# The down weights of a decoder's last feed-forward: all eleven unpacked from the start of the cross attention in front of it, ahead of the loads of the gate and up tiles

## The chip, the cores and the metric

The kernel runs on one core of a Trainium2 chip. A core has five engines with a queue of instructions each, which run in the order of their queues and wait for one another by semaphores: TensorE (PE, matrix products and transposes), VectorE (DVE), ScalarE (ACT), GpSimd (POOL) and SyncE (SP, which here only issues the transfers between memory and the core's buffers). The metric is the device time of one execution in microseconds, and lower is better: the median of several executions, 1584.54 us for the kernel before (three executions, 1584.25 to 1585.16).

## The reference, cut to what matters

A decoder of two layers with post-norm works on four batches of 512 rows by 512 columns in float32. Six stages follow one another, and each ends with a residual sum and a layer norm. The change touches the weights of the sixth stage, and moves their preparation beside the fifth.

```python
def _L1_xattn_ref(hidden_states, memory_tokens, memory_mask):        # stage E
    scores = jnp.einsum('bsd,bmd->bsm', hidden_states, memory_tokens) * scale
    scores = jnp.where(memory_mask[:, None, :], scores, neg_inf)
    attn = jax.nn.softmax(scores, axis=-1)
    readout = jnp.einsum('bsm,bmd->bsd', attn, memory_tokens)
    ...

def _dequant_fp4(packed_i32, scales_f16, group_size):                # group_size 128
    nib = w[:, :, None] >> shifts & jnp.uint32(15)
    vals = _FP4_LUT[nib.astype(jnp.int32)].reshape(out_f, in_p * 8)
    s_full = jnp.repeat(s, group_size, axis=1)
    return vals * s_full

def _L1_ffn_ref(x, gate_up_packed, gate_up_scales, down_packed, down_scales):   # stage F
    w_gu = _dequant_fp4(gate_up_packed, gate_up_scales, GROUP_SIZE)  # 2816 x 512
    w_down = _dequant_fp4(down_packed, down_scales, GROUP_SIZE)      # 512 x 1408
    gate_up = jnp.einsum('bsh,oh->bso', x, w_gu)
    gate, up = (gate_up[..., :I], gate_up[..., I:])                  # I = 1408 = 11 x 128
    h = jax.nn.silu(gate) * up
    y = jnp.einsum('bsi,hi->bsh', h, w_down)
    rms = jnp.sqrt(jnp.mean(y * y, axis=-1, keepdims=True) + EPS)
    return y / rms

x = _layernorm(x + _L0_attn_ref(...), axis=-1)     # A
x = _layernorm(x + _L0_xattn_ref(...), axis=-1)    # B
x = _layernorm(x + _L0_ffn_ref(...), axis=-1)      # C
x = _layernorm(x + _L1_attn_ref(...), axis=-1)     # D
x = _layernorm(x + _L1_xattn_ref(x, ctx_2048, mask_BxS2_bk0), axis=-1)   # E
x = _layernorm(x + _L1_ffn_ref(...), axis=-1)      # F
```

## The kernel before

The stages are called A to F, a task is one stage on one batch (E1 is the cross attention of layer 1 on batch 1), and the tasks run in the order A0 to A3, B0 to B3, and so on to F3. Between stages the rows go through memory: `finish` stores the four normed tiles of a task and `load_x` of the next stage loads them. A tile is 128 x 512.

**What sets the order.** Every task is a Python generator that writes instructions and yields after each step. `lanes` runs two tasks at once, step by step in turn, and starts the next when one is done or far enough. A `Pipe` holds work back: `later(n, f)` calls f n ticks later, so that an instruction is written only when its input is nearly there. The weights of later stages are prepared by background generators. `BESIDE` lists them as (first task, last task, key): after every step of the lanes, `step(n)` advances each listed generator by one step, from the start of its first task until the one behind the last has been started. If a task needs a weight that its generator hasn't written yet, `need` runs the generator on until it has. A scheduler then orders the instructions of each engine from what was written, with its own idea of when each is ready. It may move them past one another. `issue_after(i)` keeps what is written under it behind instruction i. `ahead` and `between` place the scalings of stage F and its norm.

**Buffers.** Pool `op` (tag o) has 69 tiles, `tp` (t) 13, `xp` (x) 12, `wp` (w) 4. An instruction or a load that takes a buffer waits until the last reader of its former content is done. In the SP queue such a wait holds all transfers behind it.

**High and low halves.** Products are made in three matmuls from a rounded high half and the rest: `split` copies the high half on ACT (L143) and subtracts it on DVE or POOL for the low half (L146). The names end in h and l: exh and exl are the halves of E's transposed input, p4h and p4l those of an unpacked down tile.

**Stage E (`l1_xattn`).** Per batch: loads of x and of the mask; the context in both layouts (ecT for the scores, ecn for the values, low halves on POOL); the mask's penalty (L1030, L1031); transposes of x (`ex`) with their splits; scores `es` (48 matmuls, lines 154 to 156); per score tile a minimum on DVE (L1041) and an exp on ACT (L1042); transposes of the weights (`ep`), the product with the values (`pv`), residual sum (L425) and norm statistics (L211, L212); and then the norm (L220, ACT's Ln and Exp, L174 to L176, four L235) and the stores.

**Stage D's end.** `merge` (L983, L984) joins D's results per tile, their transposes are `dF`, the output projection is `dy` and its sum L1001.

**Stage F (`l1_ffn`).** Per batch and per i of 11: eight scaled products `fg` (L1185), each scaled into a sum by ACT (L1133, L1137) or DVE (L1141); silu (L1149), the product with up (L1153), a split (fhh, fhl), and the accumulation `facc` over the down tile i (L1168). The gate and up codes were unpacked earlier (`l1_ffn_codes`, beside D1 to D3, key F0) and lie in memory (`gu_codes`); the down tiles are unpacked by `l1_ffn_weights`, key F.

**`l1_ffn_weights`.** It first finishes generator F0. Then, for each i of 11, it loads two gate and up tiles `gu` (pool o) from `gu_codes`, then the scales p4s and the packed down tile dn_p. Five ticks later (`F_LOAD`) `down` unpacks: `bits` is a shift (L1074) and a mask (L1075) on DVE, L1101 multiplies by the scale on DVE, and `split` copies p4h on ACT and subtracts p4l on POOL. Both halves stay in pool o until the end of F3: 22 buffers, and the 22 gu tiles likewise. In F, `need("F", ...)` at the start of each i asks that the down tile i + 1 has been written.

Of the kernel before, what the change touches and what calls it, by code (L numbers as in the profile page):

```python
# [12 lines left out]
F16 = mybir.dt.float16  # L13
BF16 = mybir.dt.bfloat16
I32 = mybir.dt.int32
# [6 lines left out]
B, S, D = 4, 512, 512  # L22
P = 128
# [8 lines left out]
LOG_EXP = "natural_log_exp_and_others"  # L32
D_NEXT = 7
B_NEXT = 13
F_LOAD = 5
CODES_EVERY = 3
F_SCALED, F_ACT, F_PAIR, F_DOWN = 1, 5, 3, 9
ORDER = "A0 A1 A2 A3 B0 B1 B2 B3 C0 C1 C2 C3 D0 D1 D2 D3 E0 E1 E2 E3 F0 F1 F2 F3"

BESIDE = [("A1", "A3", "C0"), ("A3", "B0", ("B", 0)), ("B0", "B2", "C"), ("C3", "D0", "D"), ("D1", "D3", "F0"), ("E2", "E2", "F")]  # L40


class Pipe:
# [25 lines left out]
class Net:  # L69
# [1023 lines left out]
    def l1_ffn_weights(self):  # L1093

        yield from self.bg["F0"]
        nc, a, bits = self.nc, self.a, self.bits
        pipe = Pipe()

        def down(w, sc):
            f = bits(w)  # L1100
            nc.vector.scalar_tensor_tensor(f, f, 2.0 ** 126, sc, ALU.mult, ALU.mult)  # L1101
            self.dn.append(self.split(f, "p4", lo_eng=nc.gpsimd))

        for i in range(11):
            for u in range(2):
                pipe.tick()
                self.gu[i, u] = self.o("gu", F32R)
                self.load(self.gu[i, u].bitcast(F32), self.gu_codes[i * 2 + u])
                yield
            pipe.tick()  # L1110
            sc = self.load(self.t("p4s", F16), a["dn_s"][i : i + 1, :].to_broadcast([P, 512]))
            pipe.later(F_LOAD, down, self.load(self.w("p4", I32), a["dn_p"][i]), sc)
            yield
        yield from pipe.drain()

    def l1_ffn(self, b):
        nc = self.nc
        pipe = Pipe()
# [57 lines left out]
            acc[t] = f  # L1176

        for i in range(11):
            self.need("F", lambda: len(self.dn) > min(10, i + 1))
            for u in range(2):  # L1180
                for g in range(4):
                    pipe.tick()
                    ps = self.pa("fg")
                    for n in range(2):
                        nc.tensor.matmul(ps, self.gu[i, u][:, g * P : (g + 1) * P], xT[g][n], start=n == 0, stop=n == 1)  # L1185
                    pipe.later(F_SCALED, scaled, i, u, g, ps)
                    yield
# [93 lines left out]
def body(tc, args, phases=range(6)):  # L1281
    with ExitStack() as ctx:
# [9 lines left out]
        def step(n):  # L1292
            if len(phases) == 6:
                for first, last, key in BESIDE:
                    if plain.index(first) < n <= plain.index(last) + 1:
# [74 lines left out]
```

## Time and profile before

| | us |
|---|---|
| median of three executions | 1584.54 (1584.25 to 1585.16) |
| the profiled execution | 1581.65 |
| its span, first to last instruction | 1580.0 |
| mean granted TensorE clock over it | 0.996 |
| PE busy, 1190 to 1280 (E1's tail to E3) | 84.03 of 90 |
| PE busy, 1280 to 1330 (F0) | 46.98 of 50 |
| L1074, L1075, L1101 each (medians of all on the tile) | 0.54, 0.49, 0.69 |
| p4h on ACT, p4l on POOL (medians) | 0.62, 1.30 |

The profile is of one execution; its times are counted from its first instruction, and the execution's own time is its span plus 1.65 us around it. E0 begins with its loads near 1137, its scores near 1144; E1's scores begin at 1183.3; F0's products run from about 1281. The unpacking of the eleven down tiles is spread from 1057 (first L1074) to 1321 (end of the last p4l).

In the views, a line of the timeline is start, length, engine, line of the kernel, operation, and out<-in by the program's names; brackets hold the idle time in front of it and what ended it. PEclk is the clock that the chip granted to TensorE, as a share of full speed. An engine that is not the one that the others wait for may idle for nothing.

### The profile page before, as it was taken

Reading aid. Unit: us, or ns where it says so; the run is one execution under the profiler, and the core shown is the slowest. Engines: PE = TensorE matmul, PEld = TensorE weight load, DVE = VectorE, ACT = ScalarE, POOL = GpSimd, SP = SyncE. Lnnn points to the kernel's source line nnn. Section 1 sums busy time; section 2 is a strip of 40 time slices with the busy share of each in tenths; the row PEclk is TensorE's granted clock in tenths of the full one; section 3 lists DMA queues with packets and bytes.
Section 4 is the critical chain, followed back from the end, with each engine's and each line's share of the span. In section 5 each row is a group of like instructions: output and inputs, shape, how many; then the busy total and the mean of one; then the engine's idle time right before and its main releaser. Section 6 shows DMA issues by size and latency. Waiting matters only on the chain.

```text
span 1580.0 us, 25595 instructions
## 1 busy us (share of the span) xinstructions
PE 1515.4 (96%) x8222; PEld 1090.1 (69%) x8222; DVE 1232.9 (78%) x2658; ACT 1021.3 (65%) x2208; POOL 666.2 (42%) x672
## 2 busy tenths in 40 slices
PE   8999999999999999899999999999999999999996
PEld 6888786444544674477777668777687777777875
DVE  6486589999976688777577797767786888888896
ACT  5333336988878877888696864969634445545554
POOL 6673663555535303430435323353225344344342
PEclk9999999999999999999999999999999999999998
DMA  7043344455214744653434445633436630020101
GB/s 255 29 157 124 113 154 132 149 173 176 78 48 123 224 137 133 201 185 134 134 102 118 104 141 148 171 97 92 125 123 222 233 110 12 24 81 1 54 1 53
DMA packets 134150, 192.31 MB, mean 122 GB/s; under 512 B 17265, under 2 KB 52081, under 8 KB 134017
## 3 DMA queue, kind: packets, MB, share of 16 engines
q1 hardware_dynamic: 129888, 182.23, 36.3%
q0 software_dynamic: 4128, 8.46, 2.2%
q8 instruction: 65, 1.06, 0.3%
q14 instruction: 69, 0.56, 0.1%
HBM read 117.75 MB, written 47.71 MB: 105 GB/s over the span
## 4 chain that ended last, share of the span: by engine, by line
PE 63%; DVE 17%; ACT 8%; issue 6%; DMA 3%; POOL 3%; SPq 0%; ACTq 0%; DVEq 0%; POOLq 0%
PE fg L1185 7%; PE facc L1168 5%; PE dT L933 3%; DVE fg L1141 3%; PE pg L687 3%; PE had L755 2%; PE dn L741 2%; DVE bsm L474 2%; PE pu L689 2%; ACT de L923 2%; PE bo L498 2%; PE do L953 2%; PE qk L156 2%; PE qk L155 2%; PE qk L154 2%
## 5 line engine op out<-in xcount | busy, mean ns | idle before, releaser
L1141 DVE SCALAR_TENSOR_TENSOR fg<-fg,gs,fg 128x512 f32<-128x512 f32 x220 | 163.2, 745 | 30.9 <-ACT fg L1133 15.3
L923 ACT ACTIVATE de<-de,dm 128x128 f32<-128x128 f32 (+3 forms) x256 | 142.9, 563 | 11.3 <-DVE dm L919 10.9
L1185 PE MATMUL fg<-fxh,gu 128*128 128x512 f32 x352 | 140.2, 398 | 6.1 <-DVE fg L1141 3.1
L919 DVE CUSTOM_DVE_ANT_0 de<-ds,negm,thr 128x128 f32<-128x128 f32 (+3 forms) x256 | 126.4, 546 | 19.4 <-PE ds L908 16.0
L482 POOL TENSOR_SCALAR be<-be,bsm 128x512 f32<-128x512 f32 x128 | 96.5, 766 | 103.8 <-DVE bsm L480 72.7
L1185 PE MATMUL fg<-fxl,gu 128*128 128x512 f32 x352 | 137.4, 390 | 0.1
L664 POOL TENSOR_TENSOR hl<-g,hh 128x512 fp32r<-128x512 f32 x64 | 83.4, 1309 | 110.2 <-ACT hh L663 90.2
L1145 POOL TENSOR_TENSOR fg<-fg,fg 128x512 f32<-128x512 f32 x44 | 60.2, 1367 | 139.6 <-DVE fg L1141 60.0
L476 ACT ACTIVATE be<-bs,bsm 128x512 f32<-128x512 f32 x128 | 87.3, 690 | 31.1 <-DVE bsm L474 29.2
L845 POOL TENSOR_TENSOR dql<-dqf,dqh 128x512 fp32r<-128x512 f32 x32 | 41.4, 1295 | 150.8 <-ACT dqh L844 150.6
L933 PE MATMUL dT<-ident,de 128*128 128x128 f32 x640 | 92.0, 280 | 8.5 <-ACT de L923 6.4
L933 PEld LDWEIGHTS dT<-ident,de 128*128 128x128 f32 x640 | 72.3, 142 | 28.3 <-ACT de L923 14.0
L1185 PEld LDWEIGHTS fg<-fxh,gu 128*128 128x128 f32 x352 | 66.0, 188 | 30.1 <-DVE fg L1141 12.7
L474 DVE TENSOR_REDUCE bsm<-bs 128x1 f32<-128x512 f32 x128 | 83.4, 672 | 0.0
L498 PE MATMUL bo<-bpT,cT 128*64 128x512 f32 x256 | 76.7, 618 | 2.4 <-ACT bpT L489 1.2
L248 PEld LDWEIGHTS bT<-ident,be 128*128 128x128 f32 x512 | 54.9, 141 | 34.0 <-issue 11.5
L248 PE MATMUL bT<-ident,be 128*128 128x128 f32 x512 | 73.2, 281 | 3.6 <-POOL be L482 2.1
L1185 PEld LDWEIGHTS fg<-fxl,gu 128*128 128x128 f32 x352 | 66.1, 188 | 12.8 <-DVE fxl L146 0.4
L352 POOL TENSOR_TENSOR z<-z,rope_cos 128x512 f32<-128x512 f32 x32 | 46.8, 1473 | 64.8 <-DVE zs L349 57.8
L1133 ACT ACTIVATE fg<-fg,gs 128x512 f32<-128x512 f32 x88 | 60.1, 684 | 20.6 <-PE fg L1185 20.4
L687 PE MATMUL pg<-qT,tb 128*128 128x512 bf16 x256 | 66.8, 381 | 4.5 <-ACT qT L649 2.8
L1159 POOL TENSOR_TENSOR fhl<-fg,fhh 128x512 fp32r<-128x512 f32 x44 | 58.5, 1331 | 29.5 <-ACT fhh L1158 29.3
(355 smaller groups left out, 4640.3 us busy)
## 6 DMA issues: line engine op xcount, KB each, us to landing
x<-x SPq DMA_DIRECT2D x176, 256.0 KB, 3.0
had_scratch<-hw SPq DMA_DIRECT2D x64, 256.0 KB, 2.3
z<-had_scratch SPq DMA_DIRECT2D x64, 256.0 KB, 5.8
stk<-dqh SPq DMA_DIRECT2D x192, 64.0 KB, 2.1
tw<-in_wg_t SPq DMA_DIRECT2D x32, 256.0 KB, 3.8
tw<-in_wu_t SPq DMA_DIRECT2D x32, 256.0 KB, 3.7
tw<-in_wd_t SPq DMA_DIRECT2D x32, 256.0 KB, 2.8
p<-in_gu_p SPq DMA_DIRECT2D x22, 256.0 KB, 3.1
```

What stands on the lines that cost most here:

```text
L248: self.nc.tensor.transpose(pt[:, i * P : (i + 1) * P], srcs[i][:, j * P : (j + 1) * P], self.ident)
L474: nc.vector.tensor_reduce(sm[:, h : h + 1], ps, AX.X, ALU.max, negate=True)
L476: nc.scalar.activation(e, ps, AF.Exp, bias=sm[:, h : h + 1], accum_out=sm[:, 2 + h : 3 + h])
L482: nc.gpsimd.tensor_scalar(es[h][i], es[h][i], sm[:, 4 + h : 5 + h], 1.0, ALU.mult, ALU.mult)
L498: nc.tensor.matmul(po[0][h * 64 : h * 64 + 64, :], cT[j][:, c : c + 64], pTs[h], start=j == 0, stop=j == NT - 1)
L664: nc.gpsimd.tensor_tensor(lo, g, hi.bitcast(F32), ALU.subtract)
L687: nc.tensor.matmul(pg, tern["wg_t"][k, c][:, m], qT[k], start=k == 0, stop=k == NT - 1)
L919: nc.vector.tensor_tensor_reduce(es[i], ps, self.negm[:, 384 - P * i :], -1.0, self.thr[:, i : i + 1], ALU.add, ALU.min, n4[:, i : i + 1])
L923: nc.scalar.activation(es[i], es[i], AF.Exp, bias=n4[:, i : i + 1], scale=-1.0, accum_out=den[:, hh * 4 + i : hh * 4 + i + 1])
L933: nc.tensor.transpose(pt[:, o + (i - j) * P : o + (i - j + 1) * P], es[i][:, j * P : (j + 1) * P], self.ident)
L1141: self.emitted["DVE"] = nc.vector.scalar_tensor_tensor(y[u], ps, s, y[u], ALU.mult, ALU.add)
L1185: nc.tensor.matmul(ps, self.gu[i, u][:, g * P : (g + 1) * P], xT[g][n], start=n == 0, stop=n == 1)
```

## The change

The generator for F's weights begins when E0 begins (before: E2) and is advanced until F0 has begun (before: until E3 has). It first loads and unpacks all eleven down tiles, one in two steps, with the unpacking two ticks behind the load (before: five), and no dn_p load is placed ahead of the instruction `self.stacked`, the last stacking transfer of D's projections written so far. When all are unpacked it loads the 22 gu tiles. In F, `need` now asks for the gu tile (i + 1, 1) instead of the down tile i + 1.

```diff
-F_LOAD = 5
...
-BESIDE = [..., ("D1", "D3", "F0"), ("E2", "E2", "F")]
+BESIDE = [..., ("D1", "D3", "F0"), ("E0", "E3", "F")]
...
         for i in range(11):
+            pipe.tick()
+            with self.tc.issue_after(self.stacked.ins):
+                w = self.load(self.w("p4", I32), a["dn_p"][i])
+            pipe.later(2, down, w, self.load(self.t("p4s", F16), a["dn_s"][i : i + 1, :].to_broadcast([P, 512])))
+            yield
+            pipe.tick()
+            yield
+        yield from pipe.drain()
+        for i in range(11):
             for u in range(2):
-                pipe.tick()
                 self.gu[i, u] = self.o("gu", F32R)
                 self.load(self.gu[i, u].bitcast(F32), self.gu_codes[i * 2 + u])
                 yield
-            pipe.tick()
-            sc = self.load(self.t("p4s", F16), a["dn_s"][i : i + 1, :].to_broadcast([P, 512]))
-            pipe.later(F_LOAD, down, self.load(self.w("p4", I32), a["dn_p"][i]), sc)
-            yield
-        yield from pipe.drain()
...
         for i in range(11):
-            self.need("F", lambda: len(self.dn) > min(10, i + 1))
+            self.need("F", lambda: (min(10, i + 1), 1) in self.gu)
```

`down`, `bits` and `split` are the same in both. So are the numbers of instructions on every engine: PE 8315, DVE 2643, ACT 1772, POOL 677, SP 840.

More of the change, by code (lines that the diff above doesn't have):

```diff
@@ L38 @@
 ORDER = "A0 A1 A2 A3 B0 B1 B2 B3 C0 C1 C2 C3 D0 D1 D2 D3 E0 E1 E2 E3 F0 F1 F2 F3"
-BESIDE = [("A1", "A3", "C0"), ("A3", "B0", ("B", 0)), ("B0", "B2", "C"), ("C3", "D0", "D"), ("D1", "D3", "F0"), ("E2", "E2", "F")]
+BESIDE = [("A1", "A3", "C0"), ("A3", "B0", ("B", 0)), ("B0", "B2", "C"), ("C3", "D0", "D"), ("D1", "D3", "F0"), ("E0", "E3", "F")]
 class Pipe:
```

## The prediction

> **What bounds the kernel now.** First the page: the share of each engine, then the chain of work that ended last.
>
> ```profile
> PE 1515.4 (96%) x8222; PEld 1090.1 (69%) x8222; DVE 1232.9 (78%) x2658; ACT 1021.3 (65%) x2208; POOL 666.2 (42%) x672
> ...
> PE 63%; DVE 17%; ACT 8%; issue 6%; DMA 3%; POOL 3%; SPq 0%; ACTq 0%; DVEq 0%; POOLq 0%
> ```
>
> TensorE is busy for 1515.4 of 1580.0 us, so all the time that any reordering can win lies in its idle 65 us, and a wait that it meets adds in full. The change touches the stretch from the last batch of the second self attention (D3) through the second cross attention (E0 to E3) to the first batch of the last feed-forward (F0). So next the busy times in ten-microsecond windows there (columns: window, length, PE, PEld, DVE, ACT, POOL busy with counts, granted clock, DMA share, GB/s).
>
> ```profile
> 1120.00:1130.00 10.00, 9.36 (x84) 6.91 (x82) 8.44 (x33) 9.05 (x29) 0.00 (x0) 1.00 0.03 7
> 1130.00:1140.00 10.00, 9.10 (x52) 4.01 (x52) 6.82 (x17) 4.82 (x14) 5.09 (x6) 0.83 0.65 230
> 1140.00:1150.00 10.00, 8.57 (x54) 7.07 (x54) 8.80 (x12) 4.71 (x9) 5.90 (x4) 1.00 0.91 284
> 1150.00:1160.00 10.00, 10.00 (x51) 8.23 (x50) 8.63 (x18) 7.26 (x16) 5.23 (x4) 1.00 0.24 84
> 1160.00:1170.00 10.00, 10.00 (x51) 8.32 (x50) 7.20 (x17) 0.59 (x1) 0.00 (x0) 1.00 0.01 2
> 1170.00:1180.00 10.00, 10.00 (x50) 8.40 (x49) 9.79 (x19) 3.01 (x7) 2.72 (x2) 1.00 0.33 113
> 1180.00:1190.00 10.00, 9.95 (x53) 8.15 (x52) 9.63 (x19) 4.42 (x10) 5.09 (x4) 1.00 0.51 179
> 1190.00:1200.00 10.00, 8.22 (x47) 6.40 (x45) 3.06 (x9) 4.85 (x11) 3.39 (x3) 1.00 0.93 317
> 1200.00:1210.00 10.00, 8.94 (x40) 6.95 (x41) 6.17 (x13) 8.89 (x18) 8.28 (x8) 1.00 1.02 380
> ...
> sum 210.00, PE 197.99 PEld 153.49 DVE 172.88 ACT 103.28 POOL 85.86; mean PE 9.43 PEld 7.31 DVE 8.23 ACT 4.92 POOL 4.09
> ```
>
> The reader is to see three things. PE idles 1.78 and 1.06 us in the two windows from 1190, while DVE has 6.94 and 3.83 us to spare. DVE is full from 1170 to 1190 (9.79 and 9.63), just before that idle time. And over 1120 to 1190, DVE has 70 - 59.31 = 10.7 us free in all. In F0, a window from 1280 to 1330 shows PE busy 46.98 of 50, an idle 3.02 us; the two stretches of 50 us behind it show only 0.25 and 0.46. Which operations PE waits for, from 1120 to 1340 (us in total, times, longest):
>
> ```profile
> PE ep L248 <- ACT ee L1042: 2.6, 5, 1.1
> PE dT L933 <- ACT de L923: 1.5, 3, 0.7
> PE es L154 <- DVE exl L146: 1.5, 2, 1.3
> PE fg L1185 <- ACT fg L1133: 1.3, 2, 0.9
> PE dF L248 <- DVE do L984: 1.2, 1, 1.2
> PE fg L1185 <- DVE fg L1141: 1.2, 2, 0.9
> ```
>
> Last, the timeline of DVE and ACT in these places (start, length, engine, line, operation, with the idle time before it):
>
> ```profile
> 1183.37 0.68 DVE L146 TENSOR_TENSOR exl<-ex,exh 128x512 fp32r<-128x512 f32 x1
> 1189.31 1.92 DVE L235 TENSOR_SCALAR x<-x,ln 128x512 f32<-128x512 f32 x4
> 1200.14 0.69 DVE L146 TENSOR_TENSOR exl<-ex,exh 128x512 fp32r<-128x512 f32 x1 [7.08 <-ACT exh L143]
> 1195.12 1.27 ACT L143 CAST ecnh<-ecn 128x512 fp32r<-128x512 f32 x2 [7.96 <-DMA ecn<-in_ctx]
> 1317.29 1.63 DVE L1101 SCALAR_TENSOR_TENSOR p<-p,p4s 128x512 f32<-128x512 f32 x1
> ```
>
> E1's first exl, the low half of its transposed input, starts at 1183.37 and PE's first score matmul that reads it at 1184.10: it is just in time. E1's tail then stalls on ACT, which stands for 7.96 us behind a late ecn load. In F0 an unpack step L1101 takes 1.63 us between the scaling steps L1141 that PE needs.
>
> **The change, part by part.** Nothing is added or removed: the instruction counts of all engines are equal, and only places change.
>
> *One set.* Unpacking one down tile costs, by the medians of the unpack tile p, DVE 0.541 (L1074) + 0.485 (L1075) + 0.689 (L1101) = 1.71 us, ACT 0.62 (p4h) and POOL 1.30 (p4l). Start to start, where they run back to back, the three DVE steps take 0.44 + 0.40 + 0.61 = 1.45.
>
> *What comes into 1120 to 1190 on DVE.* Before, the bit steps of tiles 1 to 4 ran at 1057.5 to 1066, their L1101 at 1158.9 to 1163.7, and tiles 5 to 11 from 1209.8 to 1317.3. In the changed program's order all 11 stand between D3's softmax and E1's first exl. So DVE gets 4 x 1.03 + 7 x 1.71 = 16.1 us (13.5 start to start) into a stretch with 10.7 us free: at least 16.1 - 10.7 = 5.4 must overflow (2.8 by the short durations). If only the larger gaps can be used (1.5 in 1120 to 1130, 2.6 between L1031 and the first L983 at 1141, 2.8 in 1160 to 1170) it is 16.1 - 6.9 = 9.2.
>
> *Where the overflow lands.* Three sets stand right in front of E1's exh and exl, with E0's layer norm (L220, ACT's Ln and Exp, L174 to L176), and E0's four L235 now come ahead of exl 2 to 4 instead of behind all four. Queued behind them on DVE are all of E1's scores; PE has nothing else to do there. E1's last exl ended at 1186.92, and PE read it some 1 us later (score matmuls start every 0.23 us there, the one at 1187.87 reads it at the latest); the norm and L235 in front of it, until 1191.2, are at most 4.3 - 1.0 = 3.3 more. Hence a PE delay of 5.4 to 9.2 + 3.3 = 12.5 us, or 2.8 if the short durations hold and the norm's steps fill gaps. I take **8.0**, nearer the low end, as E0 itself absorbs part of it. In this sum stands the extra L1101 ahead of E0's own second exl (0.8 us).
>
> *POOL beside DVE.* L1101 took 0.69 us alone and up to 1.63 beside POOL's work. In E0 it runs beside p4l as well, and so can stretch L235 (0.54 to 1.5). This is the reason for not taking the low end. [...]
>
> *The clock.* After the gaps around 1130 the granted clock was 0.62 in 1132 to 1134 and 0.53 in 1134 to 1136: 0.76 + 0.94 = 1.7 us lost. PE's pause at E1 may bring the same: 0 to 1.7, taken as **0.8**. [...]
>
> *What it wins.* E1's tail: the ecn loads stay where they are on SP (behind E0's x stores), while the scores come some 8 us later, so the exps are no longer late. PE idle 1.78 + 1.06 = 2.84, of which I take **2.4** back (bounds 2.0 and 2.84). E2 and E3: DVE loses the sets at 1209.8 to 1270; the PE idle there is small except 2.11 in 1250 to 1260, which has the same late ecn load as its cause and is not touched: **0.6** (0 to 2.0). F0: 3.02 idle against some 0.3 in the 50 us behind it; **2.4** (1.0 to 3.0). Together 5.4, bounds 3.0 and 7.8.
>
> *At nothing:* the bits taken out of 1057 to 1066 (PE is busy 19.98 of 20 there), and the DMAs. Eleven dn_p and p4s loads move ahead; on SP the dn_p loads 5 and 6 wait for POOL's p4l 1 and 2 to free a buffer, and E1's x and mask loads and E0's ecn loads stand behind them, at about 1150 instead of 1140. E0's ecn is used near 1174 and E1's x at 1181.7, so 24 and 30 us of cover hide it; gone, each us is one of PE. The 22 gu loads are all ahead of E3's context loads, and have until 1280.
>
> *Sum:* +8.0 + 0.8 - 5.4 = **+3.4 us** on the profiled execution (1581.65 us; span 1580.0 and 1.65 around it). That execution is 0.2% under the median of 1584.54; I carry the difference over: 1584.54 + 3.4 = **1587.9**.
>
> **The rivals.**
> *The sets fit in.* DVE's short durations hold, the gaps are filled, and exl comes 2.8 us late at most, half of it over PE's own shift in E0 (some 1.4 us of PE). Then +1.4 + 0 - 5.4 to -7.8, in the middle -5.2: 1579.3. For it: PE is 10.00 of 10 busy from 1150 to 1180, so DVE's work can slide behind it for long; F0's gain is plain in the rows. Against it: 9.79 and 9.63 from 1170.
> *A draw.* An overflow of 5 us pays for a relief of 5.4: 1584.1.
> *Late context loads*, the slower side's worse case: the 22 unpacked down tiles are held in the 69 buffers of pool o from E0 on, gu takes 22 more, and a gu load that waits for a buffer at the head of SP's queue holds E2's and E3's context loads. One such stall cost 2.84 at E1; two on top of the forecast: +3.4 + 5.7 = 9.1, 1593.6. It decides once a gu load waits until less than some 5 us before E2's scores. Against it: in the order of the changed program, the buffers that these loads reuse are freed by then.
> *It doesn't do what it says:* excluded, as the order of all queues has moved.
>
> **How the numbers follow.** Within 0.2% (3.2 us) a measurement of this kernel can't tell a change from none. Forecast 0.50, of which its spread (PE delay 5.4 to 12.5, relief 3.0 to 7.8) leaves 0.37 beyond 3.2 us and 0.13 within; late loads 0.11, slower; fit 0.32, faster; draw 0.07, same. Slower 0.48, same 0.20, faster 0.32. The forecast's own range is 1583 to 1594. For 8 in 10 it must take in most of the faster case and the late loads: 1578 to 1595.5.
>
> **What would show it.** In the changed profile: E1's first exl some 5 to 10 us after its x transposes, with PE waiting for exl as the largest wait; the clock under 1 just behind; no idle of PE on ep or ecn at E1's tail; in F0 no L1101, and PE idle under 0.8 us in its first 50. Wrong if DVE shows E1's exl in time (the sets fit), if a wait for a load stands in E2 or E3, or if F0 keeps its 3 us without any unpack step.

## The result and the profile after

The changed kernel takes 1598.65 us (median of four executions, 1597.84 to 1599.47) against 1584.39 for the kernel before in the same comparison: a ratio of 1.0093, with a 95% interval from 1.0078 to 1.0108. It is 14.3 us slower. The forecast was 3.4 us slower, with 1595.5 as the upper end of the range. The direction was right, the size was not.

The page after shows first that no engine has more to do: DVE, ACT and POOL ran 2658, 2208 and 672 instructions, as many as before, and are busy for 1.4, 0.1 and 1.7 us less. These are the busy times and the shares of the chain that ended last:

```profile
PE 1517.5 (95%) x8191; PEld 1091.1 (68%) x8222; DVE 1231.5 (77%) x2658; ACT 1021.2 (64%) x2208; POOL 664.5 (42%) x672
...
PE 59%; DVE 18%; ACT 8%; issue 7%; DMA 4%; POOL 4%; SPq 1%; ACTq 0%; DVEq 0%; POOLq 0%
```

PE is busy for 1517.5 us, 2.1 more than before, but the span grew by 16.0, from 1580.0 to 1596.0. So 13.9 of the 16.0 us are time in which PE stood, and its share of the chain fell from 63% to 59%. The windows of ten microseconds show where (columns: window, length, PE, PEld, DVE, ACT and POOL busy, granted clock, DMA share, GB/s):

```profile
1140.00:1150.00 10.00, 7.39 (x61) 5.15 (x56) 9.93 (x14) 5.85 (x11) 7.54 (x6) 1.00 0.61 205
1150.00:1160.00 10.00, 10.00 (x50) 7.77 (x51) 10.00 (x14) 2.11 (x4) 5.13 (x4) 1.00 0.64 198
1160.00:1170.00 10.00, 7.07 (x29) 4.87 (x27) 8.89 (x14) 4.15 (x8) 6.79 (x5) 1.00 0.38 132
1170.00:1180.00 10.00, 9.15 (x48) 7.77 (x49) 9.74 (x25) 5.63 (x14) 2.76 (x3) 1.00 0.23 76
1180.00:1190.00 10.00, 10.00 (x45) 8.25 (x44) 10.00 (x23) 1.95 (x6) 2.48 (x2) 1.00 0.35 121
1190.00:1200.00 10.00, 2.94 (x20) 2.31 (x19) 9.11 (x15) 3.68 (x9) 5.20 (x5) 0.82 0.75 273
1200.00:1210.00 10.00, 7.32 (x25) 5.15 (x24) 6.90 (x12) 1.69 (x4) 2.47 (x3) 0.67 0.54 184
```

DVE is busy for 57.67 of the 60 us from 1140 to 1200; before, it was 47.11. PE, which was at 10.00 from 1150 to 1180, now loses 2.93 us in 1160 to 1170, then 7.06 and 2.68 from 1190 to 1210, and there the granted clock falls to 0.82 and 0.67. PE's waits from 1120 to 1360, largest first (line numbers after are one lower than before up to the unpack generator; in the runs below that add lines they move again):

```profile
PE es L153 <- ACT exh L142: 7.1, 1, 7.1
PE dy L155 <- DVE dFl L145: 3.7, 2, 2.4
PE es L155 <- DVE exl L145: 2.7, 1, 2.7
PE dF L247 <- DVE do L983: 2.4, 1, 2.4
PE es L153 <- DVE exl L145: 1.6, 2, 1.5
PE dT L932 <- ACT de L922: 1.5, 3, 0.7
PE ep L247 <- ACT ee L1041: 1.1, 3, 0.8
PE fg L1187 <- ACT fg L1135: 0.9, 2, 0.5
```

How far PE's landmarks are behind the kernel before, from the starts of the same matmuls in the two traces:

| landmark | before, us | after, us | behind | step |
|---|---|---|---|---|
| first transposes of E0's x | 1141.15 | 1143.24 | 2.1 | 2.1 |
| E0: first dy | 1158.10 | 1162.29 | 4.2 | +2.1 |
| E0: first ep | 1166.26 | 1174.84 | 8.6 | +4.4 |
| E1: first score | 1183.34 | 1199.24 | 15.9 | +7.3 |
| E2: first transposes of x | 1194.67 | 1215.44 | 20.8 | +4.9 |
| E2: first score | 1200.89 | 1220.30 | 19.4 | -1.4 |
| F0: first fg | 1256.82 | 1275.84 | 19.0 | -0.4 |
| F1: first transposes | 1338.18 | 1354.24 | 16.1 | -3.0 |

F0's first products fg run among those of E3, so that row stands well ahead of F0's first accumulation (1282.47 before). From F1 on nothing more changes. Of the first 2.1 us, 1.5 arise around 933, ahead of every moved instruction, and are none of the change's: before, the granted clock was 1.00 from 930 to 938, after, it was 0.94 and then 0.64, behind the same short gaps of 0.64, 0.16 and 0.74 us. The other 0.5 arise between 1051 and 1079, in all seven kernels run that were made from the changed one and in none of the six made from the one before, so they belong to its order. From E0 on 14.0 us are left, and 14.5 with that, close to the 14.3 of the medians.

**E0, +2.1 and +4.4.** The timeline of DVE, POOL, SP and ACT there (SPq is SP issuing a transfer):

```profile
1146.35 1.81 DVE L1100 SCALAR_TENSOR_TENSOR p<-p,p4s 128x512 f32<-128x512 f32 x1
1148.08 1.75 DVE L983 TENSOR_TENSOR do<-do,dm 128x512 f32<-128x512 f32 x1
1144.64 6.33 POOL L145 TENSOR_TENSOR ecTl<-ecT,ecTh 128x512 fp32r<-128x512 f32 x4
1150.93 1.30 POOL L145 TENSOR_TENSOR p4l<-p,p4h 128x512 fp32r<-128x512 f32 x1
1152.25 0.33 SPq L251 DMA_DIRECT2D p<-in_dn_p  x1
1155.00 1.88 SPq L251 DMA_DIRECT2D ecn<-in_ctx  x4
1161.21 1.27 ACT L142 CAST ecnh<-ecn 128x512 fp32r<-128x512 f32 x2 [3.90 <-DMA ecn<-in_ctx]
1162.39 0.58 ACT L142 CAST dFh<-dF 128x512 fp32r<-128x512 f32 x1
1163.94 0.81 DVE L1073 TENSOR_SCALAR p<-p,i 128x512 int32<-128x512 int32 x1 [1.11 <-DMA p<-in_dn_p]
1164.67 1.48 DVE L1029 TENSOR_SCALAR pen<-mk 128x512 f32<-128x512 uint8 x1
1166.07 0.68 DVE L145 TENSOR_TENSOR dFl<-dF,dFh 128x512 fp32r<-128x512 f32 x1
```

One unpack step L1100 stands between the two steps that join a tile of D3, and takes 1.81 us (0.68 alone) as POOL computes four ecTl beside it. L983 behind it starts at 1148.08, and PE waits 2.4 us for that tile (1.2 before). Then the sixth dn_p load holds SP until 1152.25, since its buffer is free only when POOL's second p4l is done, at 1152.23. The ecn loads behind it are issued at 1155.00. ACT stands for 3.90 us until they land, with the casts dFh that E0's projection needs next in its queue. The input of the third dFh was there at 1156.23, and its cast starts at 1162.39. But it is DVE that comes last: the cast is done at 1162.97, and its dFl starts at 1166.07, behind an unpack step L1073, which stands 1.11 us for its own dn_p load, and a mask step L1029. The fourth dFl stands behind unpack steps again. So both queues make dFl late, and PE waits 3.7 us in all for the two.

**E1's scores, +7.3 and +4.9.** DVE and ACT in front of them:

```profile
1193.72 0.67 DVE L1100 SCALAR_TENSOR_TENSOR p<-p,p4s 128x512 f32<-128x512 f32 x1
1194.43 0.62 ACT L142 CAST p4h<-p 128x512 fp32r<-128x512 f32 x1 [3.99 <-DVE p L1100]
1196.65 1.22 DVE L219 TENSOR_SCALAR ln<-ln 128x4 f32<-128x4 f32 x1
1197.90 0.20 ACT L222 ACTIVATE ln<-ln 128x4 f32<-128x4 f32 x1 [2.33 <-DVE ln L219]
1198.63 0.56 ACT L142 CAST exh<-ex 128x512 fp32r<-128x512 f32 x1
1198.76 1.28 DVE L173 TENSOR_TENSOR ln<-ln 128x4 f32<-128x4 f32 x1 [0.89 <-ACT ln L223]
1202.41 0.68 DVE L145 TENSOR_TENSOR exl<-ex,exh 128x512 fp32r<-128x512 f32 x1
1203.01 1.90 DVE L234 TENSOR_SCALAR x<-x,ln 128x512 f32<-128x512 f32 x4
```

The transposes of E1's x are done at 1192.2. In ACT's queue the copy p4h of the last set comes ahead of exh and stands 3.99 us for its L1100, which ends at 1194.4. The last of E0's norm statistics come only after that, and L219 ends at 1197.9. ACT's Ln stands in front of exh too and waits 2.33 us for it; exh starts at 1198.63, and the first score at 1199.24. Then exl waits on DVE for three more steps of the norm, of 1.2 to 1.3 us each beside POOL. E1's 48 scores last 15.96 us from first to last start, 11.10 before: 2.7 of that is the wait on exl, and the other 2.2 fit the lower clock: from 1196 to 1208 it was 0.54, 0.50 and 0.68 in stretches of 4 us.

**F0, -3.0.** No unpack step is left there, and PE is busy 48.84 of 50 us, against 46.98 in the 50 us of F0 before:

```profile
1300.00:1350.00 50.00, 48.84 (x211) 38.91 (x211) 39.24 (x63) 24.74 (x41) 20.78 (x16) 1.00 0.12 42
```

### The profile page after: what moved, and what is told of

The parts are those of the page before. It is cut to its first block, busy times and chain, and to the rows that moved or that the text cites. A ratio compares the mean times of both kernels' runs of the same rounds, so it can differ in the third digit from the quotient of the medians.

```text
span 1596.0 us, 25585 instructions
## 1 busy us (share of the span) xinstructions
PE 1517.5 (95%) x8191; PEld 1091.1 (68%) x8222; DVE 1231.5 (77%) x2658; ACT 1021.2 (64%) x2208; POOL 664.5 (42%) x672
## 4 chain that ended last, share of the span: by engine, by line
PE 59%; DVE 18%; ACT 8%; issue 7%; DMA 4%; POOL 4%; SPq 1%; ACTq 0%; DVEq 0%; POOLq 0%
PE fg L1187 8%; PE facc L1170 6%; PE dT L932 3%; DVE bsm L473 2%; PE had L754 2%; PE pu L688 2%; ACT de L922 2%; PE dn L740 2%; PE pg L686 2%; PE bo L497 2%; DVE fg L1143 2%; PE do L952 2%; PE qk L155 2%; PE qk L154 2%; PE qk L153 2%
## 5 line engine op out<-in xcount | busy, mean ns | idle before, releaser
L1147 POOL TENSOR_TENSOR fg<-fg,fg 128x512 f32<-128x512 f32 x44 | 59.8, 1360 | 158.6 <-DVE fg L1143 64.5
L1135 ACT ACTIVATE fg<-fg,gs 128x512 f32<-128x512 f32 x88 | 60.2, 684 | 23.6 <-PE fg L1187 23.6
L1139 ACT ACTIVATE fg<-fg,gs 128x512 f32<-128x512 f32 x44 | 30.3, 689 | 66.5 <-PE fg L1187 66.4
```

## The experiments

Every run stands beside runs of the kernel before on one chip (medians there 1578.9 to 1580.4). As one profile may hold more dips of the clock in stages A to D than another (from 934 to 938 it was 1.00 before and 0.64 after), the table also gives the loss from E0's first transposes to the accumulations of F1, from the traces, all against the same profile of before. For the changed kernel that is 14.0. The differences of the medians lie within 2 us of that column, so two rows that differ by less are not told apart.

| run | median, us | ratio to before | loss E0 to F1, us |
|---|---|---|---|
| before, generator from E0 | 1594.83 | 1.0096 [1.0079, 1.0112] | 15.9 |
| changed, three tiles held | 1590.46 | 1.0065 [1.0043, 1.0087] | 9.3 |
| changed, ecn loads first | 1591.16 | 1.0072 [1.0057, 1.0087] | 9.5 |
| before, generator E1 to E3 | 1590.50 | 1.0065 [1.0050, 1.0080] | 10.9 |
| changed, three edits | 1588.80 | 1.0063 [1.0043, 1.0083] | 8.5 |
| changed, no p4l | 1593.71 | 1.0091 [1.0075, 1.0108] | 12.5 |
| changed, generator from E1 | 1594.01 | 1.0093 [1.0078, 1.0109] | 14.8 |
| before, generator E2 to E3 | 1583.05 | 1.0025 [1.0015, 1.0036] | 4.3 |
| changed, E0's norm behind exl | 1594.97 | 1.0101 [1.0083, 1.0119] | 13.8 |
| before, E2 to E3, behind exl | 1582.36 | 1.0012 [1.0003, 1.0021] | 1.8 |
| before, E3's ecn loads first | 1580.55 | 1.0008 [0.9999, 1.0018] | 0.8 |
| the last two together | 1581.08 | 1.0017 [1.0006, 1.0028] | 2.3 |

**Is it the start of the generator, or the order of its tiles?**

```diff
-BESIDE = [..., ("E2", "E2", "F")]       # the kernel before, all else unchanged
+BESIDE = [..., ("E0", "E3", "F")]
```

> The kernel before with one edit: its generator for F's weights starts at E0 instead of E2, and still loads two gate and up tiles ahead of each down tile. Theory (the loss comes from where the unpack steps stand in DVE's and ACT's queues in E0 and E1, not from which tiles are loaded first): the down tiles are again unpacked in E0 and in front of E1's scores, so the time is 8 to 16 us over before, some 1592 to 1600. Rival (the order, down tiles first, makes the loss, as the loads crowd SP's queue at E0): with the old order the loss is under 4 us.

The loss is about the same, 15.9 us (14.4 by the medians), so the order of the tiles doesn't make it; starting at E0 does. Its place differs, however. E0 loses 3.2 us, E1's scores start in time, and then PE waits 3.3 and 1.3 us for exl 2 and 3, in front of which sets and E0's norm now stand, and 5.3 us for E1's exps.

**Do three sets in front of E1's scores make 12 us?**

```diff
         def down(w, sc, i):
-            f = bits(w)
+            with self.tc.issue_after(self.exl[1].ins if i > 7 else self.stacked.ins):   # E1's last exl
+                f = bits(w)
...
```

The generator also pauses in front of tile 9 until that exl is written, so the loads of the last three tiles, and the gu loads, come later too.

> The changed kernel, with the unpack steps of the last three down tiles placed behind E1's last exl; the first eight stay in E0. Theory (12 of the 16 us arise at E1's scores, because exh, exl and the norm in front of them stand behind three sets): the E1 part, 7.3 + 4.9 us, goes nearly whole, E0's 6.5 us stay, and the time is 9 to 13 us under the changed kernel, 1586 to 1590. Rival (DVE is simply short of time, and E0's late start is what delays E1): less than 5 us come back, 1594 to 1598.

At the place itself the theory holds: E1's first score is no later than its transposes (5.85 us behind at both), the wait on exh is 1.0 in all of the stretch, and the scores last 12.07 us. But 4.7 us come back, not 9 to 13, which is the rival's number. The rest went a stage on: E1's tail, where PE now waits 3.1 us for the exps, loses 2.1 against before, and E3's scores and what follows, with E2's norm in between the exl steps, some 2.6.

**Is E0's projection late because of SP's queue?**

```diff
-            with self.tc.issue_after(self.stacked.ins):
+            while i == 4 and self.ecn is None:
+                yield
+            with self.tc.issue_after(self.stacked.ins if i < 4 else self.ecn.ins):   # E0's last ecn load
                 w = self.load(self.w("p4", I32), a["dn_p"][i])
...
```

> The changed kernel, with the loads of down tiles 5 to 11 placed behind E0's context loads (ecn) on SP. Theory of the SP queue (ACT's dFh casts of E0 stand behind casts of ecn, whose loads stand on SP behind a dn_p load that waits for a buffer): the wait of PE on dFl in E0's dy, 3.7 us, goes; the sets then come later, so that E1's part stays or grows by 0 to 3 us; in all 1 to 4 us under the changed kernel. Rival (dFl is late because eight unpack steps stand in front of it on DVE): the wait on dFl stays over 2.5 us and the time is that of the changed kernel within 2 us.

Largely. From the first dy to the first ep, E0 now loses 0.4 us instead of 4.4, and dFl is no longer among PE's waits. ACT casts the third dFh at 1157.80, right behind two ecnh and without a wait, where it came at 1162.39 in the changed kernel. So the rival's forecast falls. Its cause isn't parted from the other: as the loads come later, six unpack steps have also moved behind the first two dFl on DVE. The run without p4l, below, comes closer: there the same eight unpack steps stand in front of the first two dFl, SP isn't held by POOL, ACT stands 1.81 us for ecn, and PE waits 0.9 us for dFl. E1's part stays: the wait on exh is 7.4 and that on exl 2.9.

**Can the sets stand in E1's tail and E2?**

```diff
-BESIDE = [..., ("E2", "E2", "F")]       # the kernel before, all else unchanged
+BESIDE = [..., ("E1", "E3", "F")]
```

> The kernel before with one edit: its generator runs from E1 to E3 instead of in E2. In its order of instructions the sets stand behind E1's last exl, in E1's tail and in E2, and none in F0. Theory (F0 loses 3 us to unpack steps, E1's tail has DVE time to spare): F0's gain of 2 to 3 us comes, E0 and E1's start are as before, and the time is 1 to 5 us under before, 1579.5 to 1583.5. Rival (any set beside the cross attention costs what it saves): within 1 us of before or slower.

It is 10.9 us slower, so the theory's forecast fails. F0 gains its 3.0 us, E0 and E1's first score are as before. DVE's time to spare in E1's tail was real and of no use, as its timeline shows:

```profile
1196.66 0.79 DVE L1074 TENSOR_SCALAR p<-p,i 128x512 int32<-128x512 int32 x1 [7.10 <-DMA p<-in_dn_p]
1197.48 1.37 DVE L1075 TENSOR_SCALAR p<-p,i 128x512 int32<-128x512 int32 x1
1198.88 0.69 DVE L1101 SCALAR_TENSOR_TENSOR p<-p,p4s 128x512 f32<-128x512 f32 x1
1199.49 0.68 DVE L1041 CUSTOM_DVE_ANT_0 ee<-es,pen 128x512 f32<-128x512 f32 x1
```

The bits of a down tile stand in DVE's queue ahead of E1's minima L1041, and wait 7.10 us for their load. PE then waits 6.6 us for the exps. E2 loses 2.9 us more, and E3's scores 5.3, where exl stands behind E2's norm.

**Do the cures add up?** The first two edits together, and no L1101 between the steps that join a tile.

```diff
+            with self.tc.issue_after(self.merged.ins if i > 0 else self.stacked.ins):   # a L984 of D3
                 nc.vector.scalar_tensor_tensor(f, f, 2.0 ** 126, sc, ALU.mult, ALU.mult)
```

> The changed kernel with three edits together: loads of down tiles 5 to 11 behind E0's ecn loads, unpack steps of tiles 9 to 11 behind E1's last exl, and no L1101 of tiles 2 to 11 between the two steps (L983, L984) that join one of D3's tiles. Theory (the loss is a sum of single waits in in-order queues, each with its own place): E0 costs under 2.5 us against before instead of 6.5, E1's start nothing instead of 12.2, F0 gains 3, and E1's tail and E2 and E3 lose 1 to 4 as in the run that held three tiles: 0 to 4 us over before. Rival (DVE time is short whatever the place, so a wait that is taken away comes back at the next stage): more than 6 us over before, as with the run that held three tiles alone.

The rival holds: 8.5 us. E0 costs 4.2 (the joining steps still lose 2.9, as other unpack steps and POOL's work stand beside them; one L985, the L984 of before, took 1.68 us), E1's start 1.0, then E1's exps wait 4.2 us and E3 and F0's first transposes lose a further 2.5. Each cure worked where it was made, and the sum did not follow.

**Is it POOL beside DVE?** The low half of each down tile is left out, and the high half stands in its place.

```diff
-            self.dn.append(self.split(f, "p4", lo_eng=nc.gpsimd))
+            hi = self.o("p4h", F32R)
+            nc.scalar.copy(hi, f)
+            self.dn.append((hi, hi))
```

> The changed kernel without the eleven p4l on POOL: the low half of each down tile is left out, and the high half stands in its place in the products. Rival (POOL beside DVE makes the loss: L1101, L984 and L235 stretch while POOL computes): without 14 us of POOL work the loss falls by more than half, under 8 us over before. Theory (the order of DVE and ACT makes it): the loads of down tiles no longer wait for POOL, so E0's dy wins up to 4 us, but PE's wait in front of E1's scores stays above 5 us; 9 to 13 us over before.

The rival falls: 12.5 us are left of 14.0 without any p4l (14.4 by the medians). Ahead of its dy, E0 loses 3.9 us instead of 2.1, with the granted clock at 0.91 from 1130 to 1150, as in the changed kernel. From the first dy to the first ep it loses 1.2 instead of 4.4, as its loads no longer wait for POOL. E1's pause is 3.9 us on exh and then 4.3 on exl.

**The changed kernel with a later start.**

```diff
-BESIDE = [..., ("E0", "E3", "F")]
+BESIDE = [..., ("E1", "E3", "F")]
```

> The changed kernel with its generator started at E1 instead of E0. In its order four sets stand ahead of E1's exl 2 to 4, and the rest in E1's tail and in E2. Theory (each needed step behind an unpack step waits): E0 costs at most 1 us, E1's start 4 to 9, its tail 2 to 6, F0 gains 3: 5 to 12 us over before. Rival (only E0 is full; from E1 on there is time to spare): within 3 us of before.

At 14.8 us it is beyond the theory's upper end. E0 costs 1.4, the transposes and scores of E1 4.2, but E1's exps 7.4 in one wait, and F0's first transposes wait 3.1 for their loads.

**The kernel before, through E2 and E3.**

```diff
-BESIDE = [..., ("E2", "E2", "F")]
+BESIDE = [..., ("E2", "E3", "F")]
```

> The kernel before, its generator run through E2 and E3 instead of E2 alone: of the sets that stood in F0 two are left there, the others stand in E2 and E3. Theory: F0 gains 1.5 to 3 us, and E3's scores lose 1 to 6, since exl and the exps stand behind them as they did with the generator from E1: 0 to 4 us over before. Rival (late sets are cheap, as the loads are long there): 1 to 3 us under before.

As the theory had it, 4.3 us slower, with F0's 3.0 gained. All of the loss stands in E3's scores and just behind: E2's norm has come in between E3's exl steps on DVE, and PE waits 4.1 us for the second.

```profile
1237.57 0.68 DVE L146 TENSOR_TENSOR exl<-ex,exh 128x512 fp32r<-128x512 f32 x1
1238.55 1.25 DVE L174 TENSOR_TENSOR ln<-ln 128x4 f32<-128x4 f32 x1 [0.29 <-ACT ln L224]
1239.84 1.21 DVE L175 SCALAR_TENSOR_TENSOR ln<-ln 128x4 f32<-128x4 f32 x1
1241.09 1.19 DVE L176 SCALAR_TENSOR_TENSOR ln<-ln 128x4 f32<-128x4 f32 x1
1242.31 1.90 DVE L235 TENSOR_SCALAR x<-x,ln 128x512 f32<-128x512 f32 x2
1244.14 1.28 DVE L146 TENSOR_TENSOR exl<-ex,exh 128x512 fp32r<-128x512 f32 x2
```

**Sets or norm, in front of E1's scores?**

```diff
+        if phase == 4 and b == 0:
+            while 1 not in self.exl:
+                yield
+            with self.tc.issue_after(self.exl[1].ins):
+                self.ln_rsqrt(ln, phase, b)
...
```

> The changed kernel with one edit: E0's norm (L220, the Ln and Exp on ACT, L174 to L176, L235) stands behind E1's last exl, as it did in the kernel before; all eleven sets stay in front. It splits the 12.2 us at E1's scores. Theory (the sets in front make about half, the norm with its waits between DVE and ACT the other half): PE's pause in front of E1's scores falls from 7.1 to 2 to 4 us and its wait on exl under 1; with the half clock gone too, 6 to 9 of the 12.2 us come back at that place. E0's stores come later, so E1's tail and E2 may give back 0 to 4. Rival (the sets alone make it): the pause stays over 5.5 us.

The pause on exh falls from 7.1 to 4.5 us, between the two forecasts, and the wait on exl goes. The start loses 4.7 instead of 7.3, and the 48 scores last 13.32 us instead of 15.96, against 11.10 before: 5.2 of the 12.2 us were the norm's, with the clock that it cost, and 7.0 are left for the sets and the clock (0.83 from 1190 to 1200 and 1.00 from 1200 to 1210, where the changed kernel had 0.82 and 0.67). As a whole nothing is won, 13.8: E2's exps now wait 5.0 us.

**A version that might beat both.** From the run through E2 and E3: tiles 8 to 11 and E2's norm behind E3's last exl, and then E2's stores behind E3's ecn loads as well, that alone on the kernel before, and both.

```diff
+            with self.tc.issue_after(self.exl[3].ins if i >= 7 else self.stacked.ins):   # the sets
                 f = bits(w)
...
+            with self.tc.issue_after(behind.ins ...):                                    # E3's last ecn load
                 nc.sync.dma_start(self.xd[phase + 1][b, i * P : (i + 1) * P, :], ys[i])
```

> The kernel before, its generator run through E2 and E3, with two rules more: tiles 8 to 11 are unpacked behind E3's last exl, and E2's norm stands behind that too. Two sets stay in F0. Theory (in the run through E2 and E3 the only large new loss, 7.7 us up to F0's first transposes, came from E2's norm between E3's exl): that loss falls under 3 us, F0 still gains 2 to 3, and the time is 0 to 3 us under before. Rival (a wait that is taken away comes back at the exps or at F0's first transposes): 1 to 5 us over before.

> The kernel before with one edit: E2's stores stand behind E3's ecn loads on SP instead of ahead of them; the down tiles stay where they were. It tells whether the exps of E3 are late only because of that place in SP's queue. Theory: the 2.1 us that PE idles in E3's tail go, F0 is as before, and the time is 1 to 3 us under before. Rival (the loads wait for buffers, not for the stores): within 1 us of before.

> The run with the sets behind E3's exl, and with E2's stores behind E3's ecn loads too. Theory (5.6 us there went into exps that stood behind late ecn loads): that wait falls under 2 us, F0's gain stays, and the time is 1 to 5 us under before. Rival (the loads now wait behind the loads of down tiles that wait for POOL): the wait stays over 3 us and the time is 0 to 4 us over before.

None beats the kernel before. In the first, the wait on exl is gone, and PE waits 5.6 us for E3's exps. In the second, E3's tail wins 2.8 us up to the first facc of F0, as the theory had it, and F0 then loses 3.5: PE's waits on DVE's scaling (L1141 before, L1147 in this run) grow from 1.2 to 4.4 us in all. One of them (1.2) is a queue's wait again, an unpack step (L1107 in this run) that stands 2.06 us for its p4s load with four scalings behind it. In the third, the exps still come 5.6 us late. DVE has the reason (L1088 and L1089 are the shift and the mask of the unpacking in this run's numbers, L1055 is the minimum in front of the exp):

```profile
1247.20 2.92 DVE L1088 TENSOR_SCALAR p<-p,i 128x512 int32<-128x512 int32 x2
1250.04 2.88 DVE L1089 TENSOR_SCALAR p<-p,i 128x512 int32<-128x512 int32 x2
1252.85 0.68 DVE L1055 CUSTOM_DVE_ANT_0 ee<-es,pen 128x512 f32<-128x512 f32 x1
```

Four steps of bits stand ahead of the minima and take over 1.4 us each. The first of the three runs has the same four steps there, and its exp waits for a minimum as well:

```profile
1253.13 0.72 ACT L1052 ACTIVATE ee<-ee,em 128x512 f32<-128x512 f32 x1 [3.06 <-DVE em L1051]
```

The ecn loads were ahead of E2's stores in that run already (issued at 1242.31, the stores from 1245.93), and in both runs two dn_p loads hold SP for 6.1 us in front of them. So the third run's second edit moved nothing that this wait hung on, and late ecn loads were not what ended it, as the expectation had read it.

## Why the prediction was right or wrong

**Slower, at E1's scores, by the sets and the norm in front of them: right, and shown.** They were the forecast's main term. With three sets held behind exl, the pause goes; with the norm alone put behind, 5.2 of the 12.2 us go. The queue was in part another: the largest wait was to be on exl, and was on exh (7.1 us against 2.7), where ACT stood for an L1100 and for the norm.

**The step that failed is the price of the DMAs and of E0: "At nothing".** The prediction saw that dn_p loads 5 and 6 wait for POOL's p4l and hold E0's ecn loads, and hid this behind 24 us of cover, since ecn "is used near 1174". That is about when PE uses it (1170.67 before). ACT casts it from 1152.05 on, and in ACT's queue the casts stood ahead of dFh, which PE needs at once. The loads also went out at 1155.00, not at 1150, and DVE had an unpack step that waited for a dn_p load in front of dFl. Measured: 4.4 us in E0, of which the run with the ecn loads first gave back 4.0 and the run without p4l 3.2; how ACT's queue and DVE's share them stays open. The 2.1 us in front of the first dy, with the joining steps, had been priced at 0.8 as "the extra L1101". And the bits taken out of 1057 to 1066, at nothing too, go with the 0.5 us lost between 1051 and 1079.

**"I take 8.0" was too small.** It was meant to hold E0's part too. E0 and E1's first score and wait on exl came to 2.1 + 4.4 + 7.3 + 2.7 = 16.5 us, above the upper bound of 12.5. At E1 alone it was 7.3 + 2.7 = 10.0, inside the bounds; the rest is E0's 6.5. Two inputs were off. The unpack steps were priced at their medians, 16.1 us into the stretch; from 1110 to 1200 they took 8.7 + 8.4 + 6.7 = 23.8 us, of which 2.6 were there before, so 21.2. The ten of the 33 steps that ran beside a POOL instruction took 5.7 us longer in all than the medians of the others:

```profile
L1100 DVE SCALAR_TENSOR_TENSOR p<-p,p4s 128x512 f32<-128x512 f32 x11 | 8.7, 806 | 0.0
L1073 DVE TENSOR_SCALAR p<-p,i 128x512 int32<-128x512 int32 x11 | 8.4, 784 | 1.1 <-DMA p<-in_dn_p 1.1
L1074 DVE TENSOR_SCALAR p<-p,i 128x512 int32<-128x512 int32 x11 | 6.7, 625 | 0.0
```

And "E0 itself absorbs part of it" failed, since E0 lost 6.5 us of its own.

**The clock:** 0.8 taken, about 2.2 measured, beyond the bound of 1.7. The 2.2 is an estimate: what the 48 scores took longer, less the wait on exl. The granted clock was 0.82 and 0.67 over 20 us, more than the one dip that the bound was read from (0.62 and 0.53 over 4 us). PE stood for 7.06 us until 1199.24, and the clock read 1.00 in 1192 to 1196, 0.54 in 1196 to 1200 and 0.50 in 1200 to 1204.

**What it wins:** 2.4 + 0.6 + 2.4 were forecast, 1.4 + 0.4 + 3.0 measured. F0's gain, 1.9 to 3.0 us from its first accumulation to F1, is shown in every run that takes sets out of F0. E1's tail won only as long as E1's scores were late; with the scores in time, its wait came back.

**The sum:** 2.1 + 4.4 + 7.3 + 4.9 - 1.4 - 0.4 - 3.0 = 13.9 us. Put into the forecast's terms: 3.4, and 6.5 for E0, 2.0 more at E1 (10.0 for 8.0), 1.4 more for the clock (2.2 for 0.8) and 0.6 less won (4.8 for 5.4) make 13.9. The terms' own bounds, 12.5 + 1.7 - 3.0, ended at 11.2. Of the rivals, "late context loads" had the right mechanism in the wrong place: not a gu load in E2 or E3, but a dn_p load in E0. "The sets fit in" fell at once: DVE is at 9.74 to 10.00 in four of the six windows.

**What was not foreseen** is that no cure added up. The three edits together left 8.5 us, where 0 to 4 were expected and where the 4.7 and 4.5 us that two of them gave back alone would leave 4.8 of the 14.0. Every wait that was taken away came back at the next place in the cross attention where a needed step of DVE or ACT stood behind a set, a norm or a load: exh, then the exps, then E3's exl, then F0's transposes. Whether these waits are the order's alone, or DVE simply has too little time in E0 and E1 (57.67 of 60 us busy), the runs don't part. Why the scheduler's order moves E2's norm in between E3's exl in some of the runs stays open.

## What to carry to other kernels

Before moving filler work to an engine with gaps, find the next step in that engine's queue that the bounding engine needs, and ask what the filler itself waits for: 7.10 us of idle DVE were filled by a wait for a load, with the needed step behind it. Cover of a load ends where its first reader stands in an in-order queue, which may be a cast on another engine long before the product that uses it (here ACT's from 1152.05, the product at 1170.67). And price a step by its duration beside the work that will really run beside it: the median over all its places was a quarter too low here (16.1 us for 21.2).

## What the runs showed of the hardware

- The unpack step L1101 and the small steps of the norm took much longer on DVE where POOL computed beside them. L1101 took 654 to 693 ns (99 instances, fourteen profiles) where no POOL instruction ran beside it, and 658 to 1819 ns, with a median of 1166, where one did (55 instances). The three small steps of the norm, 128 x 4 elements, had a median of 161 ns alone and 670 ns beside POOL in the changed kernel, with a longest of 1283. That longest one, the L173 at 1198.76, ran beside two POOL steps ecTl of 1274 and 1272 ns.
- The same short gaps in PE's work didn't always cost the same. At the end of D's softmax, gaps of 0.64 and 0.74 us within 3 us were followed by a clock of 0.81 and 0.77 from 1130 to 1138 in the profile of before, and by 1.00 in that of the run with the generator from E1 to E3 (PE was busy for 3.10 of the 4 us from 1130 in both), which was 1.7 us ahead from there on.
